# Forty of 3125 edge tiles take their rows of y from gathers of x made during the node steps

## The chip, the cores and the metric

The kernel runs on one core of a Trainium2 chip. The core has a matrix engine (PE, with its weight loads PEld), a vector engine (VectorE, DVE), a scalar engine (ScalarE, ACT), GpSimd (POOL) and a queue engine (SyncE, SP), each with its own list of instructions. They run side by side and wait for each other through semaphores. Transfers between HBM and the on-chip memory (SBUF) are issued by SP, ACT and POOL and carried out by 16 DMA engines. Indirect transfers, which gather rows by a list of row numbers, are issued by POOL.

The metric is device time in microseconds (us). A profiled execution also has a span, from its first to its last instruction.

## The reference: one layer of a graph network

There are 12500 nodes with 160 features each and 400000 edges, sorted by destination. Cut to what matters:

```python
h = maximum(layernorm(x), 0)                  # [12500, 160]
x0, x1 = h[:, :64], h[:, 64:].reshape(n, 32, 3)
s0, y0 = x0 @ W_sc0 * a / 8, x0 @ W_l1_0 * a / 8          # a = node_attr, [n, 1]
s1, y1 = einsum(x1, W_sc1) * a / 32**.5, einsum(x1, W_l1_1) * a / 32**.5
w = silu(edge_16 @ fc_W1 / 4) @ fc_W2 / 8     # 192 weights for each edge
ys0, ys1 = y0[src], y1[src]                   # a row of y for each edge
mid0 = concat(w_a * ys0 * e0, w_d * (ys1 . e1) / 3**.5)
mid1 = concat(w_b * ys0 * e1, w_c * e0 * ys1)
z0, z1 = zeros.at[dst].add(mid0), zeros.at[dst].add(mid1)
out = x + C_S * s + C_X * (z @ W_l2) * a      # z divided by sqrt(10 * 96)
```

Each row of y depends on one row of x and one number of `node_attr` alone, so a row of y for an edge can be made from the row `x[src]` and the number `node_attr[src]`.

## The kernel before: a node stage, then a loop over edges

**Node stage (lines 257 to 359).** The nodes lie in 98 tiles of 128 rows (`NT`), worked on in 13 groups of 8 tiles (`GN`; the last has 2) and inside a group in steps of 2 tiles (`HN`). A step passes through six stages with lags between them: `center` (DVE: mean and variance of each row, then x less its mean, cut off below at zero; lines 284 to 286), `turn_rows` (PE: transposes), `out_of_psum` (ACT), `map_rows` (PE: two multiplications for each tile, with the weights of y and of s side by side), and `leave` (ACT: the results, 160 columns of y and 160 of s, multiplied by a number for each row and written to the tile `ys`). That number, `ra`, is attr divided by the standard deviation: ACT takes the root after a group's last step (line 290), DVE inverts it and multiplies by attr (`scales`, lines 298 and 299). At the end of a group ACT issues the store of y to the HBM tensor `y_d` (line 333) and POOL adds the tile of x to s into `acc`, the tile from which the output will be stored (line 334). The x of a group comes into one of four buffers (`nx`); its load waits until a buffer is free again, which takes the addition of an earlier group.

The order of the instructions of PE, ACT and DVE is written out by hand (`manual_schedule`): the loop over q takes the stages in the order in which they stand, each with its lag. POOL and SP follow their own program order. In between, `first_nodes` (lines 118 to 125) turns the destinations into numbers of windows, with one reduction across partitions on POOL, `edge_weights` (lines 221 to 228) scales weights on DVE, and after the node stage `relate` (lines 130 to 170) does the rest of the window arithmetic on DVE.

**Edge loop (lines 386 to 600).** The edges lie in 3125 tiles of 128, taken in 782 blocks of 4 tiles (`GT`). For each tile POOL issues one indirect transfer that gathers 128 rows of `y_d` by the column of `src_sb` (line 420). `load(b)` issues the four of a block 8 blocks ahead of its use (`AHEAD`), into one of 10 buffers `yg`. PE makes the weights of the edges (line 451), ACT scales them (line 371), DVE multiplies them with the gathered rows (lines 377 to 384) and builds a selection matrix (lines 482 and 484), and PE sums the products by destination window (line 502). Every third block closes a group of windows, which is turned, multiplied with the output weights and added into `acc` (lines 517 to 549). Parts of `acc` are stored when no later edge can change them.

The first gather of the loop can start only when y is in HBM. A gather also waits on the one issued eight places before it: the transfers of POOL pass through eight semaphores in turn.

Of the kernel before, what the change touches and what calls it, by code (L numbers as in the profile page):

```python
# [10 lines left out]
F32 = mybir.dt.float32  # L11
I32 = mybir.dt.int32
# [6 lines left out]
P = 128  # L19
M0 = 64  # L20
# [13 lines left out]
EG = 8  # L34
GN = 8
HN = 2
LO = D - P
EPS = 1e-5
C_S = math.sin(math.pi / 8.0)
# [4 lines left out]
def kernel(  # L44
# [37 lines left out]
    const = ctx.enter_context(tc.tile_pool(name="const", bufs=1))  # L82
    dram = ctx.enter_context(tc.tile_pool(name="dram", bufs=1, space=DRAM))
    y_d = dram.tile([N, D], F32, name="y_d")
    z_d = dram.tile([ZR, ZC], F32, name="z_d")


# [166 lines left out]

    engines = {mybir.EngineType.PE, mybir.EngineType.Activation, mybir.EngineType.DVE}
    with (
        tc.tile_pool(name="nx", bufs=4) as nx,
        tc.tile_pool(name="ny", bufs=2) as ny,
        tc.tile_pool(name="ns", bufs=3) as ns,
        tc.tile_pool(name="nd", bufs=3) as nd,  # L260
        tc.tile_pool(name="nd_pt", bufs=2, space=PSUM) as nd_pt,
        tc.tile_pool(name="nd_po", bufs=6, space=PSUM) as nd_po,
    ):
        xts, yss, mvs, ras, hs, pts, hTs, poss = ({} for _ in range(8))
        steps = [(g, n, j, min(HN, n - j)) for g, n in groups for j in range(0, n, HN)]

        def load_x(g, n):
            xt = nx.tile([P, GN, D], F32, name="xt")
            if g + n == NT and N % P:
                nc.gpsimd.memset(xt[:, n - 1, :], 0.0)  # L270
            node_dma(g, n, lambda rows, t, p: nc.sync.dma_start(xt[:p, t, :], by_tile(x[rows, :])))
            xts[g] = xt

        def center(q):

            g, n, j, m = steps[q]
            xt = xts[g]
            if j == 0:
                mvs[g] = ns.tile([P, GN, 2], F32, name="mv")
            mv = mvs[g]  # L280
            h = nd.tile([P, HN, D], F32, name="h")
            for k in range(m):
                st = ns.tile([P, 6], F32, name="st")
                nc.vector.bn_stats(st, xt[:, j + k, :])
                nc.vector.bn_aggr(mv[:, j + k, :], st)
                nc.vector.tensor_scalar(h[:, k, :], xt[:, j + k, :], mv[:, j + k, 0:1], 0.0, ALU.subtract, ALU.max)  # L286
            hs[q] = h
            if j + m == n:
                ra = ns.tile([P, GN], F32, name="ra")
                nc.scalar.activation(ra[:, :n], mv[:, :n, 1], AF.Sqrt, bias=eps)  # L290
                ras[g] = ra

        def scales(q):

            g, n, j, m = steps[q]
            if j + m == n:
                ra = ras[g]
                nc.vector.reciprocal(ra[:, :n], ra[:, :n])
                nc.vector.tensor_mul(ra[:, :n], ra[:, :n], a_sb[:, g:g + n])

        def turn_rows(q):
            m, h = steps[q][3], hs.pop(q)
            pt = nd_pt.tile([P, 2, HN, P], F32, name="pt")
            for k in range(m):
                nc.tensor.transpose(pt[:, 0, k, :], h[:, k, 0:P], ident)
                nc.tensor.transpose(pt[:, 1, k, :], h[:, k, LO:D], ident)
            pts[q] = pt

        def out_of_psum(q):
            m, pt = steps[q][3], pts.pop(q)  # L310
            hT = nd.tile([P, 2, HN, P], F32, name="hT")
            nc.scalar.activation(hT[:, :, :m, :], pt[:, :, :m, :], AF.Copy)
            hTs[q] = hT

        def map_rows(q):
            m, hT = steps[q][3], hTs.pop(q)
            poss[q] = []
            for k in range(m):
                po = nd_po.tile([P, 2, D], F32, name="po")
                nc.tensor.matmul(po[:, :, 0:M0], hT[:, 0, k, :], wn0, start=True, stop=True)  # L320
                nc.tensor.matmul(po[:, :, M0:], hT[:, 1, k, :], wn1, start=True, stop=True)
                poss[q].append(po)

        def leave(q):

            g, n, j, m = steps[q]
            if j == 0:
                yss[g] = ny.tile([P, GN, 2, D], F32, name="ys")
            ys, ra = yss[g], ras[g]
            for k, po in enumerate(poss.pop(q)):  # L330
                nc.scalar.activation(ys[:, j + k, :, :], po, AF.Copy, scale=ra[:, j + k:j + k + 1])
            if j + m == n:
                node_dma(g, n, lambda rows, t, p: nc.scalar.dma_start(by_tile(y_d[rows, :]), ys[:p, t, 0, :]))
                nc.gpsimd.tensor_add(acc[:, g:g + n, :], ys[:, :n, 1, :], xts[g][:, :n, :])
                del xts[g], yss[g], ras[g]


        LEAD = 2
        with tc.manual_schedule(engines=engines):
            for g, n in groups[:1]:  # L340
                load_x(g, n)
            nc.sync.dma_start(a_sb, attr)
            node_weights()
            for g, n in groups[1:LEAD]:
                load_x(g, n)
            nc.sync.dma_start(dst_i, dst)
            last = len(steps) - 1
            for q in range(len(steps) + 4):
                if q <= last and steps[q][2] == 0:
                    g = steps[q][0] + LEAD * GN  # L350
                    if g < NT:
                        load_x(g, min(GN, NT - g))
                if q == min(4, last):
                    nc.sync.dma_start(src_sb, src)
                    edge_weight_loads()
                if q == min(10, last):
                    first_nodes()
                for stage, lag in ((scales, 1), (leave, 4), (out_of_psum, 2), (turn_rows, 1), (map_rows, 3), (center, 0)):
# [27 lines left out]
    with (  # L386
# [1 line left out]
        tc.tile_pool(name="prod", bufs=3) as prod,  # L388
        tc.tile_pool(name="ld", bufs=2) as ld,
        tc.tile_pool(name="ev", bufs=2) as evp,  # L390
        tc.tile_pool(name="yg", bufs=10) as ygp,
        tc.tile_pool(name="hid", bufs=4) as hid,
        tc.tile_pool(name="post", bufs=2) as post,
        tc.tile_pool(name="p_w", bufs=2, space=PSUM) as p_w,
# [5 lines left out]
        def tiles_of(b):  # L400
            return list(range(b * GT, min((b + 1) * GT, T)))
# [4 lines left out]
        def load(b):  # L406
            blk = b * GT // BT
            if blk not in blocks:

                xe = ld.tile([P, 512], F32, name="xe")  # L410
                v = e16[blk * P:(blk + 1) * P, :].rearrange("(s k f) (h c) -> s h f k c", s=4, k=2, h=2)
                for s in range(4):
                    for h in range(2):
                        lo = 32 * s + FC_IN * h
                        nc.sync.dma_start(xe[lo:lo + FC_IN, :].rearrange("p (k c) -> p k c", k=2), v[s, h])
                blocks[blk] = xe
            yg = ygp.tile([P, GT, D], F32, name="yg")
            rows[b] = yg
            for k, t in enumerate(tiles_of(b)):
                nc.gpsimd.indirect_dma_start(  # L420
                    out=yg[:, k, :], out_offset=None, in_=y_d,
                    in_offset=bass.IndirectOffsetOnAxis(ap=src_sb[:, t:t + 1], axis=0))
# [133 lines left out]
                    store(FLOORS[k - 1][1] if k else 0, i)  # L556


        AHEAD = 8
        K = TG // GT  # L560
        order = tc.manual_schedule(engines={mybir.EngineType.PE, mybir.EngineType.Activation, mybir.EngineType.DVE})
        with order:
# [176 lines left out]
```

## Time and profile before

| | |
|---|---|
| median of 3 runs | 4071.85 us (4071.37 to 4071.95) |
| profiled execution, device time | 4072.09 us |
| its span | 4070.3 us, so 1.8 us lie outside it |
| mean granted clock of the matrix engine | 0.931 |
| busy: PE, DVE, ACT, POOL | 3204.7, 2890.3, 2663.3, 3003.1 us |
| first gather starts, last one ends | 139.1 us, 4052.5 us |
| gathers of the edge loop | 3125, 946 ns in the median |

How to read it: the times of instructions are counted from the start of the span. A group of instructions has a line of the program, an engine, an operation, what it writes and reads, how many there are, their busy time and mean duration, and the idle time of the engine in front of them with what ended it. Matrix instructions overlap, so a busy PE is not a full PE. POOL's busy time for an indirect transfer is the making of the transfer, not the transfer itself. The node stage is the stretch from 9 to about 139 us, the edge loop the rest.

### The profile page before, as it was taken

To read this page: it belongs to the slowest core of one execution; us is meant where nothing else is said; L and a number is where in the kernel's file an instruction comes from. 1 tells how busy PE (TensorE), PEld (TensorE's weight loads), DVE (VectorE), ACT (ScalarE), POOL (GpSimd) and SP (SyncE) were. 2 spreads that over 40 slices of the span, in tenths; PEclk is the share of its full clock that TensorE was granted. 3 is DMA by queue.
4 is the path that set the end of the run, shared out by engine and by line. 5 is a ranking of instruction groups with operands and counts; after the bars stand their busy time and mean duration, and the time that the engine had idled before them with its cause. 6 is when DMAs were issued, how large, how long until landed. Compare 5 with 4: busy or idle time off the path is not lost.

```text
span 4070.3 us, 61794 instructions
## 1 busy us (share of the span) xinstructions
PE 3204.7 (79%) x17265; PEld 2330.6 (57%) x17265; DVE 2890.3 (71%) x7409; ACT 2663.3 (65%) x9478; POOL 3003.1 (74%) x3150
## 2 busy tenths in 40 slices
PE   6588787777877888877788887778777888788787
PEld 5465555555555555555555555555555555555555
DVE  7787777777777777777776777777767767767776
ACT  5476666666666666666666666666666666666665
POOL 2677777777777777777777777777777777777776
PEclk9799999999899999999999999999999999989999
DMA  5222222222222222222222222222222222242223
GB/s 158 86 76 77 73 74 74 76 74 76 74 76 71 77 75 75 76 73 75 73 77 73 76 74 75 73 75 76 74 76 74 75 73 77 73 125 75 72 77 84
DMA packets 233170, 319.87 MB, mean 79 GB/s; under 512 B 65754, under 2 KB 182566, under 8 KB 232566
## 3 DMA queue, kind: packets, MB, share of 16 engines
q0 software_dynamic: 150000, 256.20, 23.6%
q1 hardware_dynamic: 69026, 51.24, 4.3%
q10 hardware_dynamic: 13796, 8.44, 0.7%
q8 instruction: 139, 2.28, 0.2%
q14 instruction: 209, 1.71, 0.1%
HBM read 299.62 MB, written 16.00 MB: 78 GB/s over the span
## 4 chain that ended last, share of the span: by engine, by line
DVE 26%; POOL 24%; issue 22%; DMA 22%; PE 4%; DVEq 1%; ACT 1%; SPq 0%; ACTq 0%; POOLq 0%
POOL yg L420 24%; DMA yg<-y_d,src_sb 22%; DVE tmp L379 5%; DVE tmp L377 5%; DVE pr L382 3%; DVE pr L381 3%; DVE sel L484 2%; DVE pr L384 2%; DVE acc L549 2%; DVE sel L482 1%; DVE pr L380 1%; PE pz L502 1%; DVE place L532 1%; PE pw L451 1%; DVE h L286 1%
## 5 line engine op out<-in xcount | busy, mean ns | idle before, releaser
L420 POOL DMA_INDIRECT yg<-y_d,src_sb x3125 | 2961.7, 948 | 952.8 <-issue 740.1
L502 PE MATMUL pz<-pr,sel 128*128 128x256 f32 x6250 | 1621.8, 406 | 0.5 <-DVE pr L384 0.5
L371 ACT ACTIVATE pw<-pw,ev 128x96 f32<-128x96 f32 x3125 | 985.3, 315 | 914.0 <-PE pw L451 825.4
L502 PEld LDWEIGHTS pz<-pr,sel 128*128 128x128 f32 x6250 | 1237.0, 208 | 157.9 <-issue 0.9
L451 PE MATMUL pw<-w,hT 64*128 64x192 f32 x6250 | 764.0, 365 | 714.4 <-DVE pr L384 706.9
L377 DVE TENSOR_TENSOR tmp<-yg,pw 128x384 f32<-128x384 f32 x782 | 432.7, 553 | 1025.3 <-DMA yg<-y_d,src_sb 1024.0
L451 PEld LDWEIGHTS pw<-w,hT 64*128 64x128 f32 x6250 | 519.1, 195 | 1111.6 <-DVE pr L384 963.9
L509 ACT ACTIVATE zs<-pz 32x64 f32<-32x64 f32 x3126 | 667.5, 214 | 41.3
L379 DVE TENSOR_REDUCE tmp<-tmp 128x128 f32<-128x384 f32 x782 | 463.5, 593 | 27.0
L484 DVE TENSOR_TENSOR sel<-sel,pw 128x384 f32<-128x384 f32 x782 | 432.8, 553 | 26.9
L507 ACT ACTIVATE zs<-pz 32x192 f32<-32x192 f32 x1042 | 337.0, 323 | 152.6 <-PE pz L502 130.7
L382 DVE TENSOR_TENSOR pr<-pw,yg 128x384 f32<-128x384 f32 x782 | 426.8, 546 | 0.0
L429 PE MATMUL px<-xe,w 32*128 32x512 f32 x782 | 295.5, 655 | 74.6 <-issue 66.1
L434 ACT ACTIVATE hT<-px 128x512 f32<-128x512 f32 x391 | 218.0, 595 | 166.6 <-PE px L429 158.6
L380 DVE TENSOR_TENSOR pr<-pw,yg 128x256 f32<-128x256 f32 x782 | 323.3, 413 | 0.0
L381 DVE TENSOR_TENSOR pr<-pw,yg 128x256 f32<-128x256 f32 x782 | 322.5, 412 | 0.0
L526 PE MATMUL px<-wc,za 128*128 128x96 f32 (+1 forms) x1566 | 257.6, 305 | 0.4 <-ACT za L519 0.4
L482 DVE TENSOR_TENSOR sel<-iota,pw 128x128 f32<-128x128 f32 x782 | 216.2, 277 | 46.8 <-ACT pw L372 44.4
L526 PEld LDWEIGHTS px<-wc,za 128*128 128x128 f32 x1566 | 212.1, 206 | 62.3 <-issue 46.1
L540 PE MATMUL px<-os,place 128*128 128x160 f32 x1044 | 220.1, 335 | 0.5 <-ACT os L529 0.5
L384 DVE TENSOR_TENSOR pr<-pw,tmp 128x128 f32<-128x128 f32 x782 | 217.7, 278 | 0.0
L549 DVE SCALAR_TENSOR_TENSOR acc<-px,a_sb,acc 128x160 f32 x522 | 197.6, 379 | 11.8 <-PE px L540 2.3
(86 smaller groups left out, 1539.8 us busy)
## 6 DMA issues: line engine op xcount, KB each, us to landing
yg<-y_d,src_sb POOLq DMA_INDIRECT x3125
xe<-in_e SPq DMA_DIRECT2D x784, 32.0 KB
xt<-in_x SPq DMA_DIRECT2D x12, 640.0 KB
y_d<-ys ACTq DMA_DIRECT2D x12, 640.0 KB
out<-acc SPq DMA_DIRECT2D x11, 640.0 KB
raw<-in_e SPq DMA_DIRECT2D x32, 192.0 KB
dst_i<-in_dst SPq DMA_DIRECT2D x1, 1568.0 KB
src_sb<-in_src SPq DMA_DIRECT2D x1, 1568.0 KB
```

The source lines that it names most:

```text
L371: nc.scalar.activation(pw[:, k, 0:96], pw[:, k, 0:96], AF.Copy, scale=ev[:, k, 0:1])
L377: nc.vector.tensor_tensor(tmp[:, :n, 0:3, :], y1, wt[:, :n, NW:NW + 3].unsqueeze(3).to_broadcast([P, n, 3, M1]), ALU.mult)
L379: nc.vector.tensor_reduce(tmp[:, :n, 3, :], tmp[:, :n, 0:3, :].rearrange("p t c u -> p t u c"), AX.X, ALU.add)
L380: nc.vector.tensor_mul(pr[:, :n, 192:PC], wt[:, :n, 96:160], yg[:, :n, 0:M0])
L381: nc.vector.tensor_mul(pr[:, :n, 0:M0], wt[:, :n, 0:M0], yg[:, :n, 0:M0])
L382: nc.vector.tensor_mul(pr[:, :n, 96:192].rearrange("p t (c u) -> p t c u", c=3), wt[:, :n, M0:96].unsqueeze(2).to_broadcast([P, n, 3, M1]) ...
L420: nc.gpsimd.indirect_dma_start(out=yg[:, k, :], out_offset=None, in_=y_d, in_offset=bass.IndirectOffsetOnAxis(ap=src_sb[:, t:t + 1], axis=0))
L451: nc.tensor.matmul(pw[:, k, 0:NW], hT[r, o:o + P], w2[r, :], start=True, stop=True)
L484: nc.vector.tensor_tensor(sel[:, :, 0:3, :], sel[:, :, 3:4, :].to_broadcast([P, n, 3, WN]), wt[:, :n, NW:NW + 3].unsqueeze(3).to_broadcast ...
L502: nc.tensor.matmul(pz[:, 0:PC], sels[g][:, t % TG, :, :], pr[:, k, :], start=t % WT == 0, stop=last)
L509: nc.scalar.activation(zs[:, 192 + M0 * c:192 + M0 * (c + 1)], pz[WN * c:WN * (c + 1), 192:PC], AF.Copy)
L526: nc.tensor.matmul(po[:m, lo:hi], za[:, k, :m], wc[:, k, lo:hi], start=k == 0, stop=k == 1)
```

## The change

Ten blocks of the edge loop (b = 12, 24, ..., 120: 40 edge tiles) no longer gather y. Instead, while the node stage runs, POOL gathers for each of these 40 tiles 128 rows of x (into the tile `xr`) and 128 numbers of attr (into `ar`): 80 indirect transfers. In the diff `RB` is 10 and `RS` is 12. These 40 tiles then pass through the same node steps behind the 98 node tiles, in five more groups of 8, with the y half of the weights alone (`v = 1`: 160 columns and not 320). ACT stores their rows of y in the order of the edges to a new HBM tensor `yr_d`. In the loop, `load(b)` of one of the ten blocks is one plain load from `yr_d` on SP's queue.

With this go other edits. x is loaded straight into `acc`, so that no load of x waits for a buffer; all 13 groups are issued at the start, the first in two pieces (2 and 6 tiles). `src_sb` is loaded before the second group of x, the destinations after the sixth, and the edge weights behind the last x. s is added to `acc` in place on DVE (`add_s`, one stage behind `leave`) and no longer on POOL. Six small operations on DVE work out the places in the attr table. `first_nodes` comes at step 16, not 10; its reduction on POOL stands behind the 80 gathers. The loop has 12 buffers `yg`, not 10, and looks 10 blocks ahead, not 8.

```diff
+    nr = max(0, min(RB, (NB - 1) // RS - 1))
+    RT = nr * GT
+    yr_d = dram.tile([max(RT, 1) * P, D], F32, name="yr_d")
+    def made(b):
+        return b // RS - 1 if b % RS == 0 and 0 < b <= nr * RS else None
...
+        loads = groups + [(NT + t, min(GN, RT - t)) for t in range(0, RT, GN)]
+        steps = [(g, n, j, min(HN, n - j)) for g, n in loads for j in range(0, n, HN)]
...
         def load_x(g, n):
-            xt = nx.tile([P, GN, D], F32, name="xt")
...
-            node_dma(g, n, lambda rows, t, p: nc.sync.dma_start(xt[:p, t, :], by_tile(x[rows, :])))
+            node_dma(g, n, lambda rows, t, p: nc.sync.dma_start(acc[:p, g + t.start:g + t.stop, :],
+                                                                by_tile(x[rows, :])))
+        def gather_x():
...
+            nc.vector.tensor_scalar(hi, of, 7, None, ALU.arith_shift_right)
+            nc.vector.tensor_copy(hf, hi)
+            nc.vector.tensor_copy(nf, of)
+            nc.vector.tensor_scalar(hf, hf, -float(P * NT - 1), None, ALU.mult)
+            nc.vector.scalar_tensor_tensor(nf, nf, float(NT), hf, op0=ALU.mult, op1=ALU.add)
+            nc.vector.tensor_copy(ai, nf)
+            table = attr.rearrange("p i -> (p i)").unsqueeze(1)
+            for t in range(RT):
+                c = (t // GT + 1) * RS * GT + t % GT
+                nc.gpsimd.indirect_dma_start(
+                    out=xr[:, t, :], out_offset=None, in_=x,
+                    in_offset=bass.IndirectOffsetOnAxis(ap=src_sb[:, c:c + 1], axis=0))
+                nc.gpsimd.indirect_dma_start(
+                    out=ar[:, t:t + 1], out_offset=None, in_=table,
+                    in_offset=bass.IndirectOffsetOnAxis(ap=ai[:, t // GT, t % GT:t % GT + 1], axis=0))
...
-                nc.vector.tensor_mul(ra[:, :n], ra[:, :n], a_sb[:, g:g + n])
+                nc.vector.tensor_mul(ra[:, :n], ra[:, :n], a_sb[:, g:g + n] if g < NT else ar[:, g - NT:g - NT + n])
...
+                nc.tensor.matmul(po[:, 0:v, 0:M0], hT[:, 0, k, :], wn0[:, 0:v, :], start=True, stop=True)
+                nc.tensor.matmul(po[:, 0:v, M0:], hT[:, 1, k, :], wn1[:, 0:v, :], start=True, stop=True)
...
             if j + m == n:
-                node_dma(g, n, lambda rows, t, p: nc.scalar.dma_start(by_tile(y_d[rows, :]), ys[:p, t, 0, :]))
-                nc.gpsimd.tensor_add(acc[:, g:g + n, :], ys[:, :n, 1, :], xts[g][:, :n, :])
+                if g < NT:
+                    node_dma(g, n, lambda rows, t, p: nc.scalar.dma_start(by_tile(y_d[rows, :]), ys[:p, t, 0, :]))
+                else:
+                    nc.scalar.dma_start(by_tile(yr_d[(g - NT) * P:(g - NT + n) * P, :]), ys[:, :n, 0, :])
+        def add_s(q):
+            g, n, j, m = steps[q]
+            if j + m == n and g < NT:
+                nc.vector.tensor_add(acc[:, g:g + n, :], acc[:, g:g + n, :], yss[g][:, :n, 1, :])
...
+            load_x(0, HN)
             nc.sync.dma_start(a_sb, attr)
             node_weights()
+            load_x(HN, min(GN, NT) - HN) if NT > HN else None
+            nc.sync.dma_start(src_sb, src)
+            for k, (g, n) in enumerate(groups[1:]):
                 load_x(g, n)
+                if k == 4:
+                    nc.sync.dma_start(dst_i, dst)
+            edge_weight_loads()
...
-            for q in range(len(steps) + 4):
+            for q in range(len(steps) + 5):
+                if q == min(4, last) and RT:
+                    gather_x()
-                if q == min(10, last):
+                if q == min(16, mid):
                     first_nodes()
                 for stage, lag in ((scales, 1), (leave, 4), (out_of_psum, 2), (turn_rows, 1), (map_rows, 3), (center, 0),
+                                   (add_s, 5)):
...
-        tc.tile_pool(name="yg", bufs=10) as ygp,
+        tc.tile_pool(name="yg", bufs=12) as ygp,
...
+            r = made(b)
+            if r is not None:
+                nc.sync.dma_start(yg, by_tile(yr_d[r * GT * P:(r + 1) * GT * P, :]))
+                return
...
-        AHEAD = 8
+        AHEAD = 10
```

More of the change, by code (lines that the diff above doesn't have):

```diff
@@ L36 @@
 HN = 2
+RB = 10
+RS = 12
 LO = D - P
@@ L256 @@
     with (
-        tc.tile_pool(name="nx", bufs=4) as nx,
+        tc.tile_pool(name="nr", bufs=1) as nrp,
         tc.tile_pool(name="ny", bufs=2) as ny,
@@ L263 @@
     ):
-        xts, yss, mvs, ras, hs, pts, hTs, poss = ({} for _ in range(8))
-        steps = [(g, n, j, min(HN, n - j)) for g, n in groups for j in range(0, n, HN)]
+        yss, mvs, ras, hs, pts, hTs, poss = ({} for _ in range(7))
+        loads = groups + [(NT + t, min(GN, RT - t)) for t in range(0, RT, GN)]
+        steps = [(g, n, j, min(HN, n - j)) for g, n in loads for j in range(0, n, HN)]
+        if RT:
+            xr = nrp.tile([P, RT, D], F32, name="xr")
+            ar = nrp.tile([P, RT], F32, name="ar")
@@ L267, in load_x @@
         def load_x(g, n):
-            xt = nx.tile([P, GN, D], F32, name="xt")
             if g + n == NT and N % P:
-                nc.gpsimd.memset(xt[:, n - 1, :], 0.0)
-            node_dma(g, n, lambda rows, t, p: nc.sync.dma_start(xt[:p, t, :], by_tile(x[rows, :])))
-            xts[g] = xt
+                nc.gpsimd.memset(acc[:, NT - 1, :], 0.0)
+            node_dma(g, n, lambda rows, t, p: nc.sync.dma_start(acc[:p, g + t.start:g + t.stop, :],
+                                                                by_tile(x[rows, :])))
@@ new lines, in gather_x @@
+        def gather_x():
+            hi = nrp.tile([P, nr, GT], I32, name="hi")
+            ai = nrp.tile([P, nr, GT], I32, name="ai")
+            hf = nrp.tile([P, nr, GT], F32, name="hf")
+            nf = nrp.tile([P, nr, GT], F32, name="nf")
+            of = src_sb[:, RS * GT:RS * GT * (nr + 1)].rearrange("p (r c) -> p r c", c=RS * GT)[:, :, 0:GT]
+            nc.vector.tensor_scalar(hi, of, 7, None, ALU.arith_shift_right)
[13 more added lines that the diff above has]
+                    in_offset=bass.IndirectOffsetOnAxis(ap=ai[:, t // GT, t % GT:t % GT + 1], axis=0))
@@ L274, in center, with rows_of @@
+        def rows_of(g, n):
+            return acc[:, g:g + n, :] if g < NT else xr[:, g - NT:g - NT + n, :]
         def center(q):
             g, n, j, m = steps[q]
-            xt = xts[g]
+            xt = rows_of(g, n)
             if j == 0:
@@ L316, in map_rows @@
             m, hT = steps[q][3], hTs.pop(q)
+            v = 2 if steps[q][0] < NT else 1
             poss[q] = []
@@ L319, in map_rows @@
                 po = nd_po.tile([P, 2, D], F32, name="po")
-                nc.tensor.matmul(po[:, :, 0:M0], hT[:, 0, k, :], wn0, start=True, stop=True)
-                nc.tensor.matmul(po[:, :, M0:], hT[:, 1, k, :], wn1, start=True, stop=True)
+                nc.tensor.matmul(po[:, 0:v, 0:M0], hT[:, 0, k, :], wn0[:, 0:v, :], start=True, stop=True)
+                nc.tensor.matmul(po[:, 0:v, M0:], hT[:, 1, k, :], wn1[:, 0:v, :], start=True, stop=True)
                 poss[q].append(po)
@@ L329, in leave @@
             ys, ra = yss[g], ras[g]
+            v = 2 if g < NT else 1
             for k, po in enumerate(poss.pop(q)):
-                nc.scalar.activation(ys[:, j + k, :, :], po, AF.Copy, scale=ra[:, j + k:j + k + 1])
+                nc.scalar.activation(ys[:, j + k, 0:v, :], po[:, 0:v, :], AF.Copy, scale=ra[:, j + k:j + k + 1])
             if j + m == n:
-                node_dma(g, n, lambda rows, t, p: nc.scalar.dma_start(by_tile(y_d[rows, :]), ys[:p, t, 0, :]))
-                nc.gpsimd.tensor_add(acc[:, g:g + n, :], ys[:, :n, 1, :], xts[g][:, :n, :])
@@ L335, in leave @@
-                del xts[g], yss[g], ras[g]
-        LEAD = 2
+                if g < NT:
[6 more added lines that the diff above has]
+                nc.vector.tensor_add(acc[:, g:g + n, :], acc[:, g:g + n, :], yss[g][:, :n, 1, :])
@@ L339 @@
         with tc.manual_schedule(engines=engines):
-            for g, n in groups[:1]:
-                load_x(g, n)
+            load_x(0, HN)
             nc.sync.dma_start(a_sb, attr)
             node_weights()
-            for g, n in groups[1:LEAD]:
+            load_x(HN, min(GN, NT) - HN) if NT > HN else None
+            nc.sync.dma_start(src_sb, src)
+            for k, (g, n) in enumerate(groups[1:]):
                 load_x(g, n)
-            nc.sync.dma_start(dst_i, dst)
-            last = len(steps) - 1
@@ L348 @@
-            for q in range(len(steps) + 4):
[L349 to L355, printed above, removed]
-                if q == min(10, last):
+                if k == 4:
+                    nc.sync.dma_start(dst_i, dst)
+            if len(groups) <= 5:
+                nc.sync.dma_start(dst_i, dst)
@@ L357 @@
+            edge_weight_loads()
+            last = len(steps) - 1
+            mid = len(steps) - -(-RT // HN)
+            for q in range(len(steps) + 5):
+                if q == min(4, last) and RT:
+                    gather_x()
+                if q == min(16, mid):
                     first_nodes()
-                for stage, lag in ((scales, 1), (leave, 4), (out_of_psum, 2), (turn_rows, 1), (map_rows, 3), (center, 0)):
+                for stage, lag in ((scales, 1), (leave, 4), (out_of_psum, 2), (turn_rows, 1), (map_rows, 3), (center, 0),
+                                   (add_s, 5)):
```

## The prediction

> **What bounds the kernel now.** I read the page first: the chain that ended last, then the costliest groups.
>
> ```profile
> POOL yg L420 24%; DMA yg<-y_d,src_sb 22%; DVE tmp L379 5%; DVE tmp L377 5%; DVE pr L382 3%; DVE pr L381 3%; DVE sel L484 2%; DVE pr L384 2%; DVE acc L549 2%; DVE sel L482 1%; DVE pr L380 1%; PE pz L502 1%; DVE place L532 1%; PE pw L451 1%; DVE h L286 1%
> L420 POOL DMA_INDIRECT yg<-y_d,src_sb x3125 | 2961.7, 948 | 952.8 <-issue 740.1
> L377 DVE TENSOR_TENSOR tmp<-yg,pw 128x384 f32<-128x384 f32 x782 | 432.7, 553 | 1025.3 <-DMA yg<-y_d,src_sb 1024.0
> ```
>
> The reader is to see that DVE waits 1024 us for gathered rows while POOL makes nothing but gathers: 948 ns each, and 0.30 us between two that no engine explains. POOL's share of busy time (74%) hides this, because the gap does not count as busy. The question on line 420 gives the ends:
>
> ```profile
> L420 POOL DMA_INDIRECT yg<-y_d,src_sb x3125: 942/946/3141, 139.1 to 4051.6; - x196
> ```
>
> From the first start (139.12) to the last end (4052.50) are 3913.4 us for 3125 gathers. Consecutive starts lie 1.25 us apart in the median. So the span has three parts: 139.1 us until the first gather, 3913.4 us of gathers, 17.8 us of tail (4070.3 - 4052.5). The change lengthens the first, shortens the second, leaves the third.
>
> Next, what makes the first part last, from the groups between 0 and 170 us:
>
> ```profile
> L331 ACT ACTIVATE ys<-po,ra 128x320 f32<-128x320 f32 x98 | 49.3, 530 | 31.3 <-DVE ra L299 20.5 <-PE po L321 5.9 <-PE pt L306 4.4
> L286 DVE TENSOR_SCALAR h<-xt,mv 128x160 f32<-128x160 f32 x98 | 43.9, 448 | 6.7
> L334 POOL TENSOR_TENSOR acc<-ys,xt 128x1280 f32<-128x1280 f32 (+1 forms) x13 | 36.2, 2786 | 90.2 <-ACT ys L331 90.2
> L299 DVE TENSOR_TENSOR ra<-ra,a_sb 128x8 f32<-128x8 f32 (+1 forms) x13 | 7.6, 585 | 0.4
> ```
>
> ACT waits for DVE's `ra`, POOL for ACT: DVE leads. And h has a mean of 448 ns where its median is 303: in each group one h, or one `ra`, stands until POOL's 2.9 us addition is over.
>
> **Saved: 40 gathers.** 40 x 1.25 = 50.0 us, if the loop can use it. Up to b = 120, 12 blocks must then pass in the POOL time of 11: 55/12 = 4.6 us each. When the loop starts late and finds rows waiting, its blocks begin at 175.9, 179.1, 182.6, 187.5, 190.7, 194.2 and 197.4 us: 3.6 on average. There is room, so I count all 50.0. The ten plain loads go to SP, 10 blocks ahead, behind a buffer that was released two blocks before. The xe loads behind them have slots some 8 blocks early. Hidden; were a load late, DVE would wait for it alone, about 3 us each (a y store landed in 3.4).
>
> **Added: a longer node stage.** I count DVE, first for the kernel before, as a test. Undisturbed (9.11 to 15.51 us) eight tiles take 6.4, so 0.80 each.
>
> - rows (lines 284 to 286): 98 x 0.80 = 78.4
> - the pair 298/299 with the wait for the root, from the last group (130.54 to 131.09): 13 x 0.55 = 7.2
> - `first_nodes` 6.4 (29.35 to 35.72) and weight scaling 1.7 without its hold
> - POOL's holds: 98 x (0.448 - 0.303) = 14.2; 7.6 - 13 x 0.17 = 5.4; line 226, 1.9 and not 0.2, under the reduction across partitions: 1.7
>
> Sum 115.0; from 9.1 to 131.1 are 122.0. The missing 7.0 are mostly five late roots (6.6 us of waits), of up to 2.2.
>
> Now the changed kernel: rows 138 x 0.80 = 110.4; 18 pairs 9.9; `first_nodes` and weights 8.1; the hold by the reduction 1.7; no holds by additions. New are the additions on DVE. Their cost comes from two-input operations with both inputs in SBUF: 1044 elements take 1.16 us to the next start (line 155), 3123 take 3.44 (line 161), hence 1280 about 1.42. Twelve and a small one: 17.4. Six index operations at 0.2: 1.2. Of the late roots I keep half, 3.5: ACT's round from the first `ys` of a group to the next one's is 7.2 us (26.22 to the end of an hT at 32.55, a root of 0.3, the pair), and a DVE group with its addition is now 6.4 + 0.55 + 1.42 = 8.4, so ACT has time to catch up (bounds 0 and 7.0). Sum 152.2. ACT's and PE's work on the 40 extra tiles lies beside DVE's: with 160 columns their rounds are shorter than the 7.2.
>
> DVE's start: a weight load (issued 5.38) waited for the first x, which came 4.6 us after issue; a first piece of a quarter of the size should bring the start 9.1 forward by 1.5 (bounds 0, and 2.4). So DVE ends at 7.6 + 152.2 = 159.8. Its end before, 131.1, was 8.0 ahead of the first gather (transposes, ACT's last rows, store, 0.87 of issue):
>
> ```profile
> 135.84 2.26 DMA y_d<-ys
> 138.25 0.87 issue
> 139.12 1.30 POOL yg L420
> ```
>
> The last store has now 640 KB, not 52: +0.5. First gather at 159.8 + 8.5 = 168.3, later by 29.2.
>
> **Is POOL free by then?** Its 80 gathers begin when `src_sb` is there, about 12 (issued near 5, some 2 MB ahead at the 373 GB/s moved from 10 to 20 us, and other queues). A gather of 4-byte rows is not in the trace; I take 1.25 us for it as for 640-byte rows: both carry 128 row numbers. Bounds: 0.3 (the gap alone) and 2.0. That is 100 us. Here two rules of the Trainium skill speak against the change.
>
> First, DMA: Bandwidth & Descriptors, section Anatomy of one DMA — SWDGE (gpsimd) path: about 2.0 us fixed per transfer, so small ones should be joined. By the rule, paid one after another, 80 cost 160 us. The row says 1.25: starts of gathers overlap earlier landings.
>
> Second, GPSIMD Engine Reference, section Specifications: POOL shares its SBUF interfaces with VectorE and contends with DVE instructions in a 2-port mode or with two SBUF inputs. The timeline of `relate` shows both kinds:
>
> ```profile
> 146.67 0.70 DVE L154 TENSOR_SCALAR lim<-lim 128x1044 f32<-128x1044 f32 x1
> 148.57 3.40 DVE L161 TENSOR_TENSOR drel<-drel,negb 128x3123 f32<-128x3123 f32 x1
> ...
> 147.13 1.06 POOL L420 DMA_INDIRECT yg<-y_d,src_sb  x1 [0.30 <-issue]
> 148.49 0.98 POOL L420 DMA_INDIRECT yg<-y_d,src_sb  x1 [0.30 <-issue]
> 149.78 3.02 POOL L420 DMA_INDIRECT yg<-y_d,src_sb  x1 [0.30 <-issue]
> ```
>
> The gather that starts inside line 161 ends 0.83 after it; the one that had begun before pays nothing. So a hold costs at most the rest of the DVE operation, when a gather starts in it. By the rule as full exclusion, h (138 x 0.22) and the additions take 47 us from POOL; by the row, 12 additions cost about 0.8 each and h 0.03 per gather: 12 us. The other way round nothing is seen: in the loop, line 532 (128x256, both sides SBUF) takes 346 ns in the mean, 333 at least.
>
> POOL: 12 + 100 + 12 = 124, plus about 9 for the reduction with its 5.5 us of preparation: 133, 35 us before it is needed. With the rule's 160 it is 12 + 160 + 12 + 9 = 193: POOL would come 25 after DVE, and of the saving nothing would be left (193 + 0.9 - 139.1 - 50.0 = +5). The last gathered x lands about 126; DVE reads it near 152.
>
> **The sum.** -50.0 + 29.2 = -20.8. The profiled execution has 4072.09 us, 1.8 of it outside the span and 0.24 above the median; 4072.09 - 20.8 = 4051.3, against the median 4051.0. A change below 0.2% (8 us) cannot be told from none here.
>
> **Rivals.**
>
> 1. *DVE is shorter than I count*: no late roots, additions that cost less beside POOL's gathers than I read, start at 6.7. First gather 152 to 160: 4035 to 4043. For it: the undisturbed group. Against: the half clock that PE shows after each pause (0.52 from 40 to 50 us), which delays ACT.
> 2. *The node stage drags*: the edge weights are loaded behind all x (11 MB, about 36 us of transfers with y's stores, then 15 small loads that took 10.5 before, so landed near 49), and DVE asks for them near 50; a stall there cools PE again; all roots late. First gather 178 to 190: 4061 to 4073. For it: the wor wait before was 0.9 us, close to biting.
> 3. *POOL takes DVE's place as the bound of the node stage* and the kernel is slower. It decides from the point where POOL ends after 189.1 (139.1 + 50.0): 12 + 80p + 21 = 189, p = 1.95 us per gather. At p = 2.2 the first gather comes at 209: 4092. For it: the 2.0 of the rule, 3.02 in the row above, full queues until 36 us. Against: of 3124 intervals between gathers 4 exceed 1.4 us, with DVE 71% busy beside them.
> 4. *The loop can't use the gap*: PE, at 79% with half-clock stretches, needs the time between gathers. If half is lost, -25 + 29.2 = +4: 4076. Against: 3.6 us per block at 176 to 197.
>
> **Numbers.** Forecast 0.66 (its own range 4043 to 4061), rival 1 0.10, rival 2 0.13, rival 3 0.07, rival 4 0.04. Faster by over 0.2% (below 4063.7): the forecast, rival 1 and half of rival 2: 0.83. Within: 0.07 (rest of rival 2, part of 4). Slower: 0.10. The range for 8 in 10 leaves out the far half of rival 1, rivals 3 and 4 and the end of 2: 4038 to 4066. Predicted 4051.
>
> **What would show it.** Right: 3085 gathers of y at 1.25 us apart, the first between 160 and 176; h near 303 ns in the mean; twelve additions near 1.4 us; POOL done with attr by 135; no DVE wait for `xr`, `ar` or the loads from `yr_d`; the tail 17.8. Wrong: a DVE wait for `ar`, POOL's gathers above 1.9 us in the node stage, a wait for `wor`, or more than 1.25 us between y gathers.

## The result, and the profile after

The changed kernel takes 4062.92 us in the median of 18 runs (4061.47 to 4067.83), the kernel before beside it 4071.68: a ratio of 0.9981, 95% interval 0.9973 to 0.9988, or 8.8 us faster. The direction was right and the time lies inside the range, but the gain is well short of the 20.8 us that were forecast. (In three of the five groups of runs below TensorE's granted clock was 0.77 instead of 0.93 and the kernel before itself took 5677 to 5841 us, so that from those groups only stretches of the node stage are read, and their ratios say nothing of the time at 0.93.)

The page of the changed kernel, its chain by line and its groups:

```profile
POOL yg L474 23%; DMA yg<-y_d,src_sb 21%; DVE tmp L429 5%; DVE tmp L427 5%; DVE pr L432 3%; DVE pr L431 2%; DVE acc L603 2%; DVE pr L434 2%; DVE sel L538 2%; PE pz L556 2%; DVE pr L430 2%; DVE sel L536 1%; PE pw L505 1%; PE px L483 1%; DVE place L586 1%
L474 POOL DMA_INDIRECT yg<-y_d,src_sb x3085 | 2925.3, 948 | 982.5 <-issue 745.8
L427 DVE TENSOR_TENSOR tmp<-yg,pw 128x384 f32<-128x384 f32 x782 | 432.8, 553 | 972.3 <-DMA yg<-y_d,src_sb 970.8
```

Line 474 is the old line 420, line 427 the old 377. Nothing has moved in the edge loop: 40 gathers fewer, the same 948 ns and the same gap between two, and DVE still waits 971 us for rows. The question on line 474 gives the ends:

```profile
L474 POOL DMA_INDIRECT yg<-y_d,src_sb x3085: 942/946/4062, 175.2 to 4039.1; - x193
```

The first gather starts at 175.21 where it started at 139.12, and the last ends at 4040.06 where it ended at 4052.50. The span of 4059.8 us (4070.3 before) falls into the same three parts. Beside what the sum had:

| part | before | after | difference | in the sum |
|---|---|---|---|---|
| until the first y gather | 139.1 | 175.2 | +36.1 | +29.2 |
| gathers | 3913.4 | 3864.8 | -48.5 | -50.0 |
| behind the last gather | 17.8 | 19.8 | +2.0 | 0 |
| span | 4070.3 | 4059.8 | -10.5 | -20.8 |

So 6.9 of the missing us lie in the node stage, 2.0 in the tail and 1.5 in the loop. A further 1.6 come from the profiled executions: that of after (4061.72) is 1.2 below its own median, that of before (4072.09) 0.4 above its own.

The groups of the changed kernel in its node stage, 0 to 170 us:

```profile
L304 POOL DMA_INDIRECT xr<-in_x,src_sb x40 | 48.1, 1203 | 13.7 <-issue 11.9 <-DMA src_sb<-in_src 1.8
L307 POOL DMA_INDIRECT ar<-in_attr,ai x40 | 39.3, 984 | 12.2 <-issue 11.9 <-DVE h L326 0.3
L326 DVE TENSOR_SCALAR h<-acc,mv 128x160 f32<-128x160 f32 x98 | 31.9, 325 | 6.9 <-PE po L362 0.5
L384 DVE TENSOR_TENSOR acc<-acc,ys 128x1280 f32<-128x1280 f32 (+1 forms) x13 | 18.3, 1405 | 0.0
L326 DVE TENSOR_SCALAR h<-xr,mv 128x160 f32<-128x160 f32 x40 | 14.1, 352 | 2.9
L338 DVE RECIPROCAL ra<-ra 128x8 f32<-128x8 f32 (+1 forms) x18 | 3.6, 199 | 1.2 <-ACT ra L330 0.8
L136 POOL PARTITION_ALL_REDUCE negb<-neg x1 | 3.3, 3326 | 6.1 <-DVE h L326 6.1
```

The reader is to see what the sum had right: an attr gather of 4-byte rows takes 984 ns, an x gather 1203 with its holds, the additions 1405, and h has fallen from 448 to 325 and 352. DVE waits for neither `xr` nor `ar`. POOL's 80 gathers ran from 11.24 to 122.8 us and its reduction ended at 132.2 (the sum: 133), 43 us before its next work.

### The profile page after: what moved, and what is told of

It is laid out like the page before. It is cut to its first block, busy times and chain, and to the rows that moved or that the text cites. A ratio compares the mean times of both kernels' runs of the same rounds, so it can differ in the third digit from the quotient of the medians.

```text
span 4059.8 us, 62554 instructions
## 1 busy us (share of the span) xinstructions
PE 3235.3 (80%) x17505; PEld 2347.5 (58%) x17505; DVE 2922.8 (72%) x7558; ACT 2692.2 (66%) x9543; POOL 3018.0 (74%) x3177
## 4 chain that ended last, share of the span: by engine, by line
DVE 25%; POOL 23%; DMA 21%; issue 21%; PE 5%; ACT 1%; DVEq 1%; ACTq 0%; POOLq 0%
POOL yg L474 23%; DMA yg<-y_d,src_sb 21%; DVE tmp L429 5%; DVE tmp L427 5%; DVE pr L432 3%; DVE pr L431 2%; DVE acc L603 2%; DVE pr L434 2%; DVE sel L538 2%; PE pz L556 2%; DVE pr L430 2%; DVE sel L536 1%; PE pw L505 1%; PE px L483 1%; DVE place L586 1%
## 5 line engine op out<-in xcount | busy, mean ns | idle before, releaser
L474 POOL DMA_INDIRECT yg<-y_d,src_sb x3085 | 2925.3, 948 | 982.5 <-issue 745.8
```

The lines of the kernel that those rows point to most:

```text
L474: nc.gpsimd.indirect_dma_start(out=yg[:, k, :], out_offset=None, in_=y_d, in_offset=bass.IndirectOffsetOnAxis(ap=src_sb[:, t:t + 1], axis=0))
```

## The experiments

The diffs are against the changed kernel.

**The changed kernel once more, as a measure for its neighbours.**

> The changed kernel itself, as a measure for its neighbours in this job. If the edge loop is bound by PoolE's gathers as in the profile of before: 4063 and the first y gather at 175. In the earlier jobs the kernel before took 5690 and 5840 us, at a granted TensorE clock of 0.77, and the first y gather came later by some 1.7 us for each gather that PoolE makes in the node stage (133.6 with none, 197 with 40, 337 with 120, 406 with 160); if that is so here: first gather at about 265, and 1 to 2% slower than before.

Measured: 4069.39 us beside 4078.01, ratio 0.998 (0.997 to 0.999); first y gather at 175.37, tail 19.9. This is the row for the other kernels of its group (`early_yg`, `no_add2`, `best`). In this group and in that of `rb0_c` and `ahead8` the gathers are slower: without the few long intervals they start 1.252 to 1.253 us apart in the mean, against 1.250 in the profiles of before and after. Over 3085 gathers these are 5 to 7 us, about what both kernels take longer than in the first group.

**No tile made twice, all other edits kept.**

```
-RB = 10
+RB = 0
```

> No tile is made twice; the loads of x into the output's tiles, their order and the addition on VectorE stay. Theory (VectorE sets the end of the node stage; each remade block costs it 3.5 us, each group of eight 7.05 us): five groups and the six index operations fall away, the first y gather comes at 175.2 - 35.3 - 1.2 = 138.7, 3125 gathers, so about the time before, 4070 to 4074. Rival (the gain on VectorE is eaten by something that the remade tiles bring, for instance gathers that disturb VectorE or the DMA engines beside it): without them the node stage is much shorter than 139, first gather at 120 to 130 and 4055 to 4064. Rival (the other edits cost time themselves): first gather after 142, 4075 or more.

> No tile is made twice, all other edits stay. From the node stage seen earlier (first y gather 133.6): about 5.5 us less than before, 4064 to 4069 beside a before of 4071 to 4078; then the remade rows bring 50.0 and cost about 41.6 by themselves, of which the sum had 36.5, and the other edits bring 5.5 where the sum had 7. Rival (the other edits bring nothing, the remade rows 8.8): the time of before. If the longer end (19.8 and not 17.8 us behind the last gather) belongs to the remade rows, it is 17.8 here; if to the deeper buffers, 19.8.

> No tile is made twice, all other edits stay. Theory (the node stage of this kernel was seen twice with the first y gather at 131.1 and 133.6, so 44 us before the changed kernel's 175.2, while the loop saves 48.5 to 50): 5 to 8 us less than before, minus 2 if the longer end stays; ratio 0.9985 to 0.999. Rival (the other edits bring nothing): ratio 1.0. The end behind the last gather: 17.8 if its 2 us belong to the remade rows, 19.8 if to the other edits.

The first two ran at a clock of 0.77 (ratios 0.998 and 0.9981, both intervals reach over 1); their first y gathers came at 133.6 and 131.1, between the first expectation's 138.7 and its rival's 120 to 130. The third ran at 0.93: 4071.04 us beside 4076.54, ratio 0.9986 (0.9977 to 0.9995). Its line of gathers:

```profile
L474 POOL DMA_INDIRECT yg<-y_d,src_sb x3125: 942/947/3142, 132.3 to 4049.9; - x196
```

So the other edits alone bring 5.5 us; they move the first gather from 139.1 to 132.3 (which of them does it was not taken apart). The end behind the last gather is 18.5, neither of the two values expected. The remade rows move the first gather on to 174.61 in the neighbour of the same group (`ahead8`, below): they cost 42.3 us there, and the gathers take 48.8 us less. By the sum's own terms the other edits were worth 8.2 (start 7.6, rows 78.4, 13 pairs 7.2, 8.1, 1.7, 17.4, late roots 2.5 as 13 of 18 groups' share, and 8.0 behind: 130.9 against 139.1), and the remade rows 50.0 - 37.4 = 12.6. Measured between the medians: 5.5 and, from 4071.04 to 4068.0, 3.0 (5.2 between the two profiled runs: 48.8 less 42.3 and 1.3 of longer tail). Most of the missing gain is therefore missing at the remade rows.

**DVE without the additions** (the output lacks s).

```
-                nc.vector.tensor_add(acc[:, g:g + n, :], acc[:, g:g + n, :], yss[g][:, :n, 1, :])
+                pass
```

> The twelve additions of s and the small one are left out, so the output lacks s. Theory (VectorE bounds the node stage): 13 x 1.4 = 18 us shorter, first gather at about 157 and 4045; less where ScalarE's round of 7.2 us per group (against the 7.05 that VectorE needs without the addition) takes over. Rival (the stage is bound by PoolE's gathers or by ScalarE): no more than 5 us.

> The thirteen additions of s are left out, so the output lacks s. Theory (VectorE bounds the node stage, 8.64 us a group with the addition, 7.05 without): first gather 13 to 18 us earlier, 4045 to 4050 where the loop is PoolE's. Rival (PoolE or ScalarE bounds the stage): less than 5 us.

The first ran at a clock of 0.77 (1.0132; first gather 255.2). The second: 4055.33 us, ratio 0.9942 (0.9925 to 0.9958), 14.1 less than the changed kernel beside it, a smaller gain than was expected. Its gathers, and in the same window as above the row of the reciprocal:

```profile
L474 POOL DMA_INDIRECT yg<-y_d,src_sb x3085: 942/949/4062, 163.9 to 4034.4; - x193
...
L338 DVE RECIPROCAL ra<-ra 128x8 f32<-128x8 f32 (+1 forms) x18 | 3.6, 199 | 4.7 <-ACT ra L330 3.9
```

Work taken from DVE comes back as time, so DVE leads the node stage. But of 18.3 us of additions only 11.4 come back at the first gather: a group takes 7.24 us from one `ra` to the next (77.35 to 113.57, five groups) where it took 8.64, so 1.4 as paid, and then other waits appear: 4.7 us of idle time before the reciprocal where the changed kernel beside it has 0.7, and 2.3 us for the output weights where it has none. DVE leads ACT by little.

**The gathered rows' buffers placed ahead of the node stage.** A pool is a stretch of on-chip memory from which a program takes its buffers. In the changed kernel the pool `yg` is opened behind the node stage and lies where that stage's tiles lay.

```
+    ygp = ctx.enter_context(tc.tile_pool(name="yg", bufs=12))
     before = ctx.enter_context(ExitStack())
...
-        tc.tile_pool(name="yg", bufs=12) as ygp,
```

> The buffers of the gathered rows (yg) get their place ahead of the node stage instead of in the space that its tiles leave; nothing else changes. Theory (the first y gather waits for the last yr_d store only because its buffer lies where node tiles lay; its rows are complete when the last y_d store has landed, issued at 134.5): the first gather starts at 137 to 140 and not at 175, PoolE works while VectorE makes the remade rows, and the loop finds 12 blocks gathered: 25 to 37 us faster than the changed kernel, 4026 to 4038. Rival (the wait is a true one, for yr_d): first gather at 175, 4063. Rival (VectorE is needed first anyway, and the loop begins no earlier, so PoolE stands once the buffers are full): half of it, 4043 to 4050.

Measured: 4041.14 us, ratio 0.991 (0.9893 to 0.9926), 28.3 less than the changed kernel beside it. The question on the line of gathers, and POOL's timeline where it stands:

```profile
L474 POOL DMA_INDIRECT yg<-y_d,src_sb x3085: 941/949/3138, 138.0 to 4017.4; - x193
...
204.87 0.95 POOL L474 DMA_INDIRECT yg<-y_d,src_sb  x1 [0.30 <-issue]
214.81 0.94 POOL L474 DMA_INDIRECT yg<-y_d,src_sb  x1 [8.99 <-DVE pr L435]
```

The first gather starts 2.4 us after the last y_d store was issued (135.6), while DVE makes remade rows until 166.6. Behind the gather of 204.87, the 48th, POOL has no buffer left and stands for 8.7 us, until DVE has used the first two blocks: the first buffer that is free again goes to block 12, which comes from `yr_d`. The loop's first product starts at 209.0, as in the changed kernel beside it (209.4). 37.3 us earlier, 8.7 given back: 28.6. The remade rows were thus on the path only because the first y gather waited for them.

What it waits for in the changed kernel: the chain of its profiled execution names index operations of `relate`.

```profile
166.80 1.25 DVE first L141
...
174.18 0.72 DVE lim L164
174.90 0.31 issue
175.21 1.47 POOL yg L474
```

In four kernels with the old place the first gather starts 0.31 to 0.32 us after the end of line 164 (174.89, 175.06, 174.30, 163.63; gathers 175.21, 175.37, 174.61, 163.95). But the same four start 4.56 us after the issue of the last yr_d store:

```profile
170.65 0.36 ACTq L378 DMA_DIRECT2D yr_d<-ys  x1
```

A constant distance does not tell the two apart. The trace's records of POOL's own waits do. The wait for that store ended at 174.08, when the store had just landed (174.06). The last wait, one for DVE, was over at 174.47, while line 164 ran on until 174.89. From the last wait to the gather are 0.74 us, here as in `early_yg`. So the last yr_d store is the releaser, and line 164 is a neighbour in time: the chain names the work that came last, which need not be the work that was waited for. With 5 and 15 blocks (`rb5`, `rb15`) the gather starts before line 164 has ended (197.19 and 204.76; 336.85 and 337.67), and again right after the last yr_d store has landed. The first rows of y do not need that store.

**The order of the loads.** `src_sb` behind the third group of x, and the small loads of the edge weights behind the seventh group:

```
-            nc.sync.dma_start(src_sb, src)
             for k, (g, n) in enumerate(groups[1:]):
                 load_x(g, n)
+                if k == 1:
+                    nc.sync.dma_start(src_sb, src)
                 if k == 4:
                     nc.sync.dma_start(dst_i, dst)
+                if k == 5:
+                    edge_weight_loads()
```

> src_sb is loaded behind the second and third group of x instead of ahead of them; all else as in the changed kernel. Theory (the small node weights, issued on the queue of ScalarE up to 6.2 us, landed at 11.4 because the 1.57 MB of src_sb were in the DMA engines ahead of them): VectorE's rows begin near 9, the first y gather comes 2 to 3 us earlier, 4060 to 4061; PoolE starts its gathers later and has room for it. Rival (it is the number of bytes, whatever they are, and x takes their place): VectorE starts at 11 to 12 as now, no change, 4063.

> src_sb is loaded behind the third group of x. Theory (1.57 MB in front of the small node weights keep VectorE waiting): VectorE's rows begin at 9.8 and not at 12, the first y gather 2 us earlier, ratio to before 0.0005 lower than the changed kernel's 0.998. Rival (a stall later takes it back: w2 and wor are no earlier, VectorE only waits longer for them): first gather as before, 175, no change.

> The 21 small loads of the edge weights are issued behind the seventh group of x instead of behind the last. Theory: VectorE's waits for w2 and wor (2.5 us together) go, the first y gather comes 2 to 2.5 us earlier, 4060.5. Rival (VectorE had slack there against ScalarE's and TensorE's rounds): no change; or x comes later behind them and VectorE waits for x instead, 4063 to 4066.

> The small loads of the edge weights go behind the seventh group of x. Theory (VectorE waits 2.5 us for w2 and wor): the wait goes, first y gather at 173, ratio to before 0.0006 lower than the changed kernel's 0.998. Rival (VectorE then waits elsewhere, for a late root or x): no change.

> The yg buffers placed ahead of the node stage, 13 of them (11 blocks ahead), src_sb loaded behind the third group of x, edge weights behind the seventh. Theory: the gain of the early buffers, 3 to 5 us from the two loads, and one more block gathered ahead: 4022 to 4034.

The four single ones all ran at a clock of 0.77 (1.0176, 1.0135, 1.0155, 1.0168), so what each is worth in time was not measured. The start of the node stage can be read. The timeline of the changed kernel:

```profile
3.14 0.33 SPq L392 DMA_DIRECT2D src_sb<-in_src  x1
...
5.55 0.60 ACTq L206 DMA_DIRECT2D wnr<-in_w_sc  x1
...
11.51 0.21 DVE L209 TENSOR_SCALAR wn<-wnr 128x96 f32<-128x96 f32 x1 [6.92 <-DMA wnr<-in_w_l]
```

and that of `src_late_b`:

```profile
5.56 0.60 ACTq L206 DMA_DIRECT2D wnr<-in_w_sc  x1
6.75 0.58 SPq L395 DMA_DIRECT2D src_sb<-in_src  x1
9.12 0.38 DVE L209 TENSOR_SCALAR wn<-wnr 128x96 f32<-128x96 f32 x1 [4.34 <-DMA wnr<-in_w_l]
```

DVE waits for the small weights on ACT's queue in both. With the 1.57 MB of `src_sb` issued ahead of the last of them, and not one group of x (0.64 MB) in its place, they arrive 2.4 us later; rows begin at 9.50, 9.84 and 9.76 in the three kernels with the late load (`src_late_b`, `src_late`, `best`), at 11.3 to 13.6 in all others of these groups with the early one.

`best` has both orders, the early buffers, 13 of them, and looks 11 blocks ahead: 4036.05 us, ratio 0.9896 (0.9879 to 0.9912), the fastest here though just outside the 4022 to 4034 expected, 33.3 below the changed kernel beside it and 5.1 below `early_yg`. But the two orders of loads are not what made these 5.1: DVE starts 2.6 us earlier, yet ends its rows no earlier than in `early_yg` (167.2 and 166.6 for the last h), it still waits 2.1 us for w2, only sooner, and 2.7 for late roots. The first gather comes no earlier either (137.8 and 138.0). What is smaller is POOL's stand behind the 48th gather, 6.0 us instead of 8.7:

```profile
211.90 0.94 POOL L476 DMA_INDIRECT yg<-y_d,src_sb  x1 [6.33 <-DVE pr L437]
```

With the thirteenth buffer POOL waits for DVE's first block and not for its second. The rest is within the spread of four runs each.

**The depth of the buffers undone.**

```
-        tc.tile_pool(name="yg", bufs=12) as ygp,
+        tc.tile_pool(name="yg", bufs=10) as ygp,
...
-        AHEAD = 10
+        AHEAD = 8
```

> The gathered rows have 10 buffers and run 8 blocks ahead, as before, instead of 12 and 10; all else is the changed kernel. Theory A (the longer end is the deeper buffers'): 17.8 us behind the last gather, 2 us faster, unless blocks remade in the node stage are then loaded too late. Theory B (it belongs to the other edits): 19.8, the time of the changed kernel. If the ten plain loads need the two blocks more: VectorE waits for them, about 3 us each, up to 30 us slower.

4068.0 us, ratio 0.9979 (0.997 to 0.9988): the changed kernel's own. The two more buffers are worth nothing in the old place, and the ten plain loads are early enough without them. Its tail is 19.8: the longer tail is not theirs.

**More and fewer remade blocks, and no attr.** RB set to 5, 15 and 20; and a kernel without the 40 gathers of attr, whose remade rows are scaled by other tiles' attr.

> Five blocks are made twice instead of ten. Theory: 25.0 us saved less in the loop, 17.6 us less in the node stage: first gather at about 157.5, time 4062.9 + 7.4 = 4070. Rival (the stage is bound by PoolE, 80 gathers and their holds): 40 gathers fewer take 50 us from PoolE and nothing remains of its bound, first gather at about 150 and 4063 or less.

> Fifteen blocks are made twice. Theory: VectorE gets 17.6 us more, first gather at about 193; PoolE, idle for 43 us with ten blocks, gets 40 more gathers (50 us and some holds) and is done at about 186, before it is needed; so 25.0 - 17.6 = 7.4 us faster than with ten, 4055.5. Rival (PoolE is the bound already, or becomes it here): first gather at 225 and more, 4088. Rival (the edge loop can't use the gap beyond the fifty microseconds): no gain, 4063 to 4080.

> Fifteen blocks are made twice. Theory (VectorE pays 3.5 us a block, PoolE has 43 us to spare): first y gather at about 193, 7.4 us less than the changed kernel, ratio to before 0.9963. Rival (PoolE is the bound from here on: 120 gathers at 1.39 us with holds end at 178, the reduction at 188, the first y gather behind it at 192): the same first gather within 3 us, so the time is the same; what tells them apart is whether VectorE or PoolE's reduction ends last. Rival (a gather of y that PoolE makes beside VectorE's longer stage holds it): first gather at 205 and more, no gain.

> Twenty blocks are made twice. Theory: PoolE gets 160 gathers in the node stage, 160 x 1.25 = 200 and some 20 of holds and 9 for the reduction, done at about 241 where VectorE would be done near 202 and be 8.5 from the first gather at 210; so now PoolE is the bound, the first gather comes at 241 or later, and the time is 4062.9 + 66 - 50 = 4079, or 16 more than with ten. Rival (PoolE's gathers are hidden whatever their number): first gather at 210, 4048.

> The 40 gathers of attr are left out, and the remade rows are scaled with other tiles' values, so the output is wrong in these blocks. Theory (PoolE is done 43 us before it is needed): half of PoolE's gathers go, nothing changes, 4062 to 4064. Rival (PoolE or its holds bound the stage): up to 50 us earlier, 4013 to 4050. Rival (PoolE's gathers slow VectorE): VectorE's instructions are shorter by some per cent, 3 to 8 us.

All ran at a clock of 0.77: ratios 1.0064, 1.0228, 1.0205, 1.0277 and 1.0079. None of the expected times was met, and the slope in RB at a clock of 0.93 remains unmeasured. What they show is told in the last section. That POOL is not the bound of the node stage rests on the profile of the changed kernel (43 us of idle time) and on `no_add2`, where less work for DVE alone brought the first gather forward by 11.4, not on `no_attr`.

## Why the prediction was right or wrong

**Right.** The loop used the gap: 3085 gathers, 1.25 apart in the median. DVE sets the node stage (`no_add2`). POOL's 80 gathers and the reduction ended at 132.2, within 1 us of the sum; the 2.0 us fixed that the Trainium skill (DMA: Bandwidth & Descriptors, Anatomy of one DMA) gives for one such transfer, by which the kernel would have been slower, are not paid one after another by gathers issued back to back, even of 4-byte rows: 1.27 us from start to start in the median, 1.39 with all holds. Nor did the shared interfaces of the second rule (GPSIMD Engine Reference, Specifications) exclude POOL: ten of the 80 gathers took about 2.0 us instead of 0.95, nine of them started in an addition and one just ahead of the long cast of line 129, much as the row of the trace had it. Additions 1.405 for 1.42, remade groups 7.05 for 6.95, no wait for `xr`, `ar` or the plain loads.

**Wrong, the largest piece: "a first piece of a quarter of the size should bring the start 9.1 forward by 1.5".** It went back to 11.93, 4.3 us from the 7.6 of the sum. What this step looked at did come: ACT issues the last of its small weights at 5.55 and no longer at 6.57. In the kernel before:

```profile
6.57 0.60 ACTq L195 DMA_DIRECT2D wnr<-in_w_sc  x1
...
8.77 0.21 DVE L198 TENSOR_SCALAR wn<-wnr 128x96 f32<-128x96 f32 x1 [2.46 <-DMA wnr<-in_w_l]
```

But from this issue to the use of the weights were 2.2 us before; now they are 6.0, and 3.6 in `src_late_b`. I looked at the first weight's wait for x, and not at the last one, and I costed the move of `src_sb` to the front of SP's queue for POOL alone. Its bytes are under way together with the small loads: from 6 to 8 and from 8 to 10 us the DMA engines are busy for 0.63 and 0.71 of the time before, for 1.00 and 0.91 in the changed kernel. What I forgot is not SP's queue or POOL's but the DMA engines that ACT's queue shares with SP's. The order of loads shows 2.4 us of the 4.3; the rest, with x issued at once, was not taken apart.

**Wrong, DVE's sum: 152.2, measured 154.8** (11.93 to 166.69). Missing was DVE's wait for w2:

```profile
53.44 0.26 DVE L232 TENSOR_SCALAR w<-w 128x192 f32<-128x192 f32 x1 [2.28 <-DMA wor<-in_w_l]
```

I had such a wait as rival 2 and gave it no share of the forecast; the kernel before waited 0.9 for the loads just behind these, and now all of them were behind all of x. In `rb0_c` that wait is 0.2 us, since there the reduction holds line 339 just ahead (1.95 instead of 0.17); with 80 gathers in front of it on POOL the reduction comes at 128.9 and holds two h of the remade rows instead (1.65 and 0.91). So the remade rows moved a hold, and uncovered a wait. The late roots, for which 3.5 were kept, cost 1.2 and just pay for it. What is left over lies in the groups: one with an addition takes 8.64 us, where the sum's terms give 6.4 + 0.55 + 1.42 = 8.37. Part of that is the other way round of the holds, of which the prediction saw nothing: while POOL gathers, two h in most groups take 0.39 us instead of 0.30. In `rb0_c`, without these gathers, none does, and a group takes 8.53.

**Right in size and in path, and never asked for: "+8.5 to the first gather".** 166.69 to 175.21 are 8.5, and they are what the sum took them for: PE, ACT, the last store and its landing. But the sum let the remade rows end before POOL may start, and never asked why it should. `early_yg` shows that they need not, and that this wait is worth 28 us, more than everything else here. With the buffers in another place the whole longer stage lies beside gathers, and only 8.7 us of it come back, as POOL's stand.

**Wrong: "Tail 17.8 unchanged".** It is 19.7 to 19.9 in all kernels at 0.93 that gather attr. The compute is the same; POOL's last `DRAIN`, an instruction at the end of the program, takes 7.49 us instead of 4.24. It starts 11.4 us behind the last gather (11.3 before) and now ends after SP's last store, which used to end 1.3 us behind it: 3.25 - 1.3 = 2.0. In `rb0_c` the drain is 4.24 again, yet the tail 18.5, since SP's last store ends 0.6 us later behind the last gather than before; why was not found.

**Wrong in size: 50.0 from the gathers, 48.5 measured.** 1.2 of it: `relate` now meets the first gathers with lines 166 and 172, and the second gather starts 4.36 us before the third; the long intervals are 7.9 us over 1.25 in all, instead of 6.7. The rest is spacing.

**The rivals.** Rival 1 fell: the late roots did shrink, but the start was later, not earlier. Rival 2 was half true: its wait for w2 and its half clock (granted clock 0.50 and 0.51 from 51 to 57.8 and from 139.7 to 146.6 us) were there, and the result lies in its 4061 to 4073, but with a first gather at 175 and not at 178 to 190, and 4.3 of the 6.9 us came from the start, which it did not have. Rivals 3 and 4 fell: 1.39 us per gather in the node stage and not 1.95, and an even spacing in the loop from the first blocks on.

**What stays open.** The 1.2 us between the profiled run and the median: the changed kernel's 18 runs spread over 6.4 us, those of before over 2.0, and the profiles show no difference that explains it. What each order of loads is worth alone.

## What to carry to other kernels

Where a change lengthens a stage that the next one waits for, ask what the wait is for before costing the stage: a pool opened behind a stage can lie in that stage's memory, and its first user then waits for work whose data it doesn't need; here moving one line was worth three times the change. When a load is moved, look for the small loads on other queues that will now be under way with its bytes, and for the wait that ends last, not the first in the list. A wait that is short in the profile may be short because a hold stands in front of it; move the hold, and it shows. And where two candidates for a releaser keep the same distance in every run, distance proves neither: look at the queue's own waits, or at a run in which they part.

## What the runs showed of the hardware that was not expected

**POOL's last drain grows with the number of attr gathers made in the node stage, some 4 ms earlier.** With 0, 20, 40 and 60 of them (RB 0, 5, 10, 15) it takes 4.24, 5.86, 7.49 and 9.13 us, the same to 0.01 us in each of the kernels, at either clock where both were run, 0.081 us for each gather of 4-byte rows; with 40 gathers of x and none of attr (`no_attr`) 4.23. With 80 (RB 20) it is 2.10. Why was not found.

**At a clock of 0.77 other things than the clock were slow, in the node stage only beside POOL's gathers.** In `rb0_b`, which gathers nothing there, the node stage goes as at 0.93 until the first y gather (131.1, against 132.3 in `rb0_c`). In the kernels that gather in the node stage ACT, PE and DVE stand for most of the time while POOL gathers, and move on when it has finished. The groups of `rb15` from 20 to 180 us, and 20 us of its windows (busy us of PE, PEld, DVE, ACT and POOL, clock, share of DMA, GB/s):

```profile
L307 POOL DMA_INDIRECT ar<-in_attr,ai x60 | 56.8, 947 | 18.3 <-issue 18.3
L373 ACT ACTIVATE ys<-po,ra 128x320 f32<-128x320 f32 x12 | 6.2, 526 | 136.8 <-remote 135.2 <-DVE ra L339 1.6
...
60.00:80.00 20.00, 3.25 (x12) 2.74 (x12) 0.00 (x0) 1.01 (x2) 15.15 (x16) 0.50 0.13 33
```

ACT makes 12 rows of `ys` in 160 us, and what releases it is nothing that the profile names, with DMA engines 13% busy. The first y gather comes the later the more gathers were made: at 131 to 134 us with none, 197 with 40 (219 with 40 and all 138 tiles), 255 to 271 with 80, 336 to 337 with 120, 406 with 160. In that condition every kernel with remade rows was slower than before (1.006 to 1.028), and the one without was not. Two chips showed both conditions, in groups of runs less than an hour apart. What brings it about is open; this change gains in one condition and loses in the other.
